# First layer's norms with operands in PSUM, and a scheduler with new durations and offsets

## The chip, the cores and the metric

The kernel runs on one core of a Trainium2 chip. A core has five engines that run their own instruction streams and meet only at semaphores: PE (TensorE, matrix products), DVE (VectorE), ACT (ScalarE), POOL (GpSimd) and SP (SyncE, which here issues nearly all DMAs). The metric is the device time of one execution in microseconds (us), as a median of several runs.

## The reference

Four images of 512 channels and 32 x 32 positions pass two layers, each added to its input:

```python
x = x + mamba(group_norm(x))      # layer 0
x = x + pab(group_norm(x))        # layer 1
```

Layer 0 takes each image as a sequence of 1024 tokens. It norms over the channels of a token, projects 512 channels to 2 x 1024, runs a causal convolution with four taps and a SiLU on one half, and from it makes `dt` (softplus), `B` and `C` (16 states each). The scan is, for each of 1024 channels and 16 states,

```python
h = exp(dt * A) * h + (dt * x) * B
y = sum over the states of h * C
```

and `(y + x * D) * silu(z)` is projected back to 512 channels. Layer 1 makes two 1x1 convolutions to 64 channels, a softmax over the whole 1024 x 1024 map, a 3x3 convolution that the map is applied to, and a last 3x3 convolution. All is float32. Both group norms have 32 groups of 16 channels.

## The kernel before, in words

Layer 0 works on tiles of 128 channels by 1024 tokens. A unit is one batch, one of eight channel tiles `d`, one of 16 states `s`: 512 units in all (function `unit`). In a unit with an even state, ACT scales the transposed `dtx` (= `dt * x`) by `B` and PE turns it into `u` in PSUM; with an odd state, SP loads the row of `B` to all partitions (`bbc`, L755) and POOL multiplies (L760). ACT makes `da = exp(dt * A)` (L739, L766), DVE scans (L774), POOL multiplies by the row of `C` (`cbc`, L786; for four states DVE does, L781), and PE adds the product into `y` (L794). So POOL has 640 products of 128x1024, and `dtx` (L689). It also transforms the weights of layer 1 in 32 filling pieces (`transform`, L1054 to L1074; ACT scales, L1046 and L1047; SP loads and stores).

Around the units stand, per batch: `norms` (both norms in one chain), `conv1` (projection `pxm`, ACT tap L584, DVE taps L593, SiLU), `gates` (`pz`, SiLU, stored to DRAM), `params` (`B`, `C`), `delta` (`dt`, `dtx`), `gate` (`pyb`, L832, L835), and `out_proj` for the batch before (loads `gt`, `wpr`, `res`; groups `po` on PE; L874). The last batch has `last_proj` instead, and `first_image` loads, norms and pads the first image for layer 1.

The norms chain: `bn_stats` on DVE; a matmul averages the means in a group (`pm`); `mid` makes the deviation; a matmul averages it (`pv`); ACT takes Ln and Exp (L247, L248) into `rstd`; `shift` makes `nb` (L444) and the matrix `mw` (L448); a matmul makes the mean shift, which is taken from `nb` (L464). Then per half of 512 tokens: group `pmu`, its DVE step (L487), ACT's squares (`sq`, L501), the group `pvar`; at last Ln and Exp (L517, L521) into `rs`, the DVE step L528 and ACT's scale and bias (L536).

The order of all this is not written out. Each piece of work is a `step` with an engine, a duration that is written in the code, what it reads and writes, and a priority (its due unit). `Plan.issue` runs a model of the five engines over these numbers and issues on each engine the ready step of lowest priority among those that can start soonest (`SLACK`); buffers come from rings with a fixed count of slots (`mm`: two PSUM buffers for all projections, turns and norms; `h` 4, `bb` 5, `cbc` 4, `wpr` 2, `res` 2, `xs` 10). `HOP` is what passes between engines, `LOAD` an ACT table load, `AHEAD` how far a filling step may run ahead. The offsets in `PRM` are due units relative to a batch: `m0` and `n0` for the norms of batch 1 and of 2 and 3, with `nl` between their parts, `q0`/`qg` and `c0`/`cg` for the convolutions of batch 1 and of 2 and 3, `e0`/`eg` and `g0`/`gg` for the gates, `o0`/`og` for the output projection, `dl` for `delta`, `fi` for the first image. A due unit decides the order alone; on the chip each engine then runs its list strictly in order.

Layer 1 has no plan: its 3x3 convolutions are matmuls over transformed weights (`m_b`, `m_o`, L1349), with `pat` and `psc` for the map.

Of the kernel before, what the change touches and what calls it, by code (L numbers as in the profile page):

```python
# [10 lines left out]
ALU = mybir.AluOpType  # L11
# [19 lines left out]
PRM = dict(fi=-0.55, m0=45.75, n0=43.74, nl=2.01, q0=54.7, qg=6.23, c0=54.63, cg=6.71, p0=120.47, e0=6.16, eg=3.72, g0=78.98, gg=9.04, o0=4.96, og=3.78, dl=8.57, t0=10, tg=20)  # L31
# [24 lines left out]
class Plan:  # L56
# [4 lines left out]
    HOP, LOAD, SLACK, AHEAD = 0.1, 1.28, 0.08, 16.23  # L61
# [41 lines left out]
    def issue(self):  # L103
# [6 lines left out]
        while left:  # L110
# [4 lines left out]
            for e in self.ENGINES:  # L115
                urgent = min((s.prio for s in ready[e] if s.table in (None, table)), default=1e9)
                found = []
                for s in ready[e]:
# [3 lines left out]
                    if s.fill and e == "DVE":  # L122
                        t = max(t, clock["POOL"])
# [25 lines left out]
            s.done = clock[s.eng] = t + s.us  # L149
            if s.fill and s.eng == "DVE":  # L150
                clock["POOL"] = max(clock["POOL"], s.done)
# [10 lines left out]
            for u in s.users:  # L162
                u.unmet -= 1
                hop = self.HOP if u.eng != s.eng or s.kb else 0.0
                u.ready = max(u.ready, s.done + hop)
                if not u.unmet:
                    ready[u.eng].append(u)
# [4 lines left out]
def mamba_then_pab_kernel(  # L172
# [76 lines left out]

    image = {}  # L250
# [5 lines left out]
    with ExitStack() as l0:  # L256
# [72 lines left out]
        MM, TR = 0.93, 0.145  # L329
# [46 lines left out]
        def norms(b, prio, lag=0.0):  # L376
# [14 lines left out]
            for c in range(NCC):  # L391

                def stats(c=c):
                    if c == 0:
                        spl["mv"] = tiny("mv", [P, NCC, 2])
                    bs = spool.tile([P, NH, 6], F32, tag="bs", name=f"bs_l0_{b}_{c}")
                    for h, hs in enumerate(halves):
                        nc.vector.bn_stats(bs[:, h, :], t()[:, c, hs])
                    nc.vector.bn_aggr(spl["mv"][:, c, :], bs)

                step("DVE", 1.6, stats, [t], [stat], prio)
# [10 lines left out]
            def mid():  # L412
                mv = spl["mv"]
                spl["mean"], spl["dev"] = tiny("gmean", [P, NCC]), tiny("gdev", [P, NCC])
                mean, dev = spl["mean"], spl["dev"]
                nc.vector.tensor_copy(mean, pm()[:, :NCC])
                nc.vector.tensor_sub(dev, mv[:, :, 0], mean)
                nc.vector.tensor_mul(dev, dev, dev)
                nc.vector.tensor_add(dev, dev, mv[:, :, 1])

            step("DVE", 0.8, mid, [pm], [stat], prio)
# [10 lines left out]
            def root():  # L432
                spl["rstd"] = tiny("grstd", [P, NCC])
                rsqrt(spl["rstd"], pv()[:, :NCC])

            step("ACT", 0.6, root, [pv], [stat], prio, "ln")

            mw = buf("res", [P, T], f"mw_{b}")  # L440

            def shift():
                spl["nb"] = tiny("gnb", [P, NCC])
                nc.vector.scalar_tensor_tensor(  # L444
                    spl["nb"], spl["mean"], -1.0, spl["rstd"], ALU.mult, ALU.mult
                )
                for c in range(NCC):
                    nc.vector.tensor_scalar_mul(  # L448
                        mw()[:, c * P : (c + 1) * P], mean_w, spl["rstd"][:, c : c + 1]
                    )  # L450

            step("DVE", 1.1, shift, [], [stat, mw], prio)

            def shift_mean():
                for c in range(NCC):
                    nc.tensor.matmul(
                        pv()[:, NCC : NCC + 1], mean_w, spl["nb"][:, c : c + 1],
# [3 lines left out]
            step("PE", 1.2, shift_mean, [stat], [pv], prio)  # L461
            step(
                "DVE", 0.3,
                lambda: nc.vector.tensor_sub(  # L464
                    spl["nb"], spl["nb"], pv()[:, NCC : NCC + 1].to_broadcast([P, NCC])
# [3 lines left out]
            rs = buf("xs", [P, L], f"rs_{b}")  # L469
            by_half = [buf(None, None, "") for h in range(NH)]  # L470
            by_chunk = [buf(None, None, "") for c in range(NCC)]
            for h, hs in enumerate(halves):
# [4 lines left out]
                            lambda c=c: mw()[:, c * P : (c + 1) * P],  # L477
# [6 lines left out]
                for c in range(NCC):  # L484
                    step(
                        "DVE", 0.7,
# [7 lines left out]
            for h, hs in enumerate(halves):  # L494
                prio += lag
                pvar = buf("mm", [P, T], f"pvar_{b}_{h}")
                for c in range(NCC):
                    sq = buf("res", [P, T], f"sq_{b}_{h}_{c}")
                    step(
                        "ACT", 0.63,  # L500
# [14 lines left out]
            def logs():  # L515
                for hs, pvar in zip(halves, pvars):
                    nc.scalar.activation(rs()[:, hs], pvar(), AF.Ln, bias=eps)  # L517

            step("ACT", 1.35, logs, pvars, [rs], prio, "ln")
            step(  # L520
                "ACT", 1.15, lambda: nc.scalar.activation(rs(), rs(), AF.Exp, scale=-0.5),  # L521
                [], [rs], prio, "exp",
            )
            prio += lag
            for c in range(NCC):
                step(
                    "DVE", 1.22,
                    lambda c=c: nc.vector.scalar_tensor_tensor(  # L528
                        t()[:, c, :], t()[:, c, :], spl["nb"][:, c : c + 1], rs(),
                        ALU.add, ALU.mult,  # L530
                    ),
                    [rs, *by_half], [by_chunk[c]], prio, holds=[t],
                )
                step(
                    "ACT", 1.15,
# [30 lines left out]
        def conv1(b, d, prio):  # L566
# [5 lines left out]
            for at, end in ((0, 341), (341, 682), (682, L)) if b else ((0, L),):  # L572
# [15 lines left out]
                step("ACT", 0.18 + n / 1000, tap, [p], [u], prio)  # L588
# [10 lines left out]
                step("DVE", 0.3 + n / 250, taps, [p], [u], prio)  # L599
            step(  # L600
                "ACT", 1.15,
# [4 lines left out]
        def gates(b, d, prio):  # L606
# [3 lines left out]
            for h, hs in enumerate(halves):  # L610
                p = project(b, NDC + d, w, f"pz_{b}_{d}_{h}", hs, prio)
                step(
                    "ACT", 0.62,
# [4 lines left out]
                "ACT", 1.15, lambda: nc.scalar.activation(sz(), sz(), AF.Silu),  # L618
# [7 lines left out]
        def params(b, prio):  # L626
# [3 lines left out]
            for h, hs in enumerate(halves):  # L630
                pp = buf("mm" if b else f"y{h}", [P, T], f"pp_{b}_{h}")
                for d in range(NDC):
# [10 lines left out]
                    "ACT", 0.58,  # L643
# [9 lines left out]
            def turn():  # L653
# [9 lines left out]
                "DVE", 0.3, lambda: nc.vector.tensor_copy(bt(), pt()[:, :, RK : RK + NS]),  # L663
# [3 lines left out]
        def delta(b, d, prio):  # L667
# [4 lines left out]
            for h, hs in enumerate(halves):  # L672
# [4 lines left out]
                    "ACT", 0.62,  # L677
# [6 lines left out]
                "ACT", 1.15, lambda: nc.scalar.activation(dt(), dt(), AF.Softplus),  # L684
# [4 lines left out]
            step("POOL", 2.38, lambda: nc.gpsimd.tensor_mul(dtx(), dt(), u()), [dt, u], [dtx], prio)  # L689
            dtxt = buf("dtxt", [P, NT, P], f"dtxt_{b}_{d}")  # L690
            for h in range(NH):
                pt = buf("mm", [P, NK, P], f"pdt_{b}_{d}_{h}")

                def turn(h=h, pt=pt):
# [8 lines left out]
                    "ACT", 0.59,  # L703
# [5 lines left out]
        def unit(b, d, s, y):  # L709
# [13 lines left out]
            if s in B_ON_ACT:  # L723
# [3 lines left out]
                for j in range(2):  # L727
# [8 lines left out]
                    step("ACT", 1.24, rows, [dtxt, bt], [sc], prio)  # L736
                step(
                    "ACT", 1.14,
# [12 lines left out]
            else:  # L751
# [8 lines left out]
                    "POOL", 2.38, lambda: nc.gpsimd.tensor_mul(dbx(), dtx(), b_bc()),  # L760
# [4 lines left out]
                    "ACT", 1.12,  # L765
# [7 lines left out]
                "DVE", 2.28,  # L773
# [5 lines left out]
            if on_dve:  # L779
                step(  # L780
                    "DVE", 1.22, lambda: nc.vector.tensor_mul(hc(), ht(), c_bc()),  # L781
                    [ht, c_bc], [hc], prio,
                )
            else:
                step(
                    "POOL", 2.38, lambda: nc.gpsimd.tensor_mul(hc(), ht(), c_bc()),  # L786
# [15 lines left out]
        def gate(b, d, y):  # L802
# [11 lines left out]
            for h, hs in enumerate(halves):  # L814
                step(
                    "ACT", 0.59,
# [3 lines left out]
            for h, hs in enumerate(halves):  # L820
# [16 lines left out]
                step("DVE", 1.45, mul, [u, sz], [p, g], prio + 2)  # L837
# [8 lines left out]
        def out_proj(b, h, prio, gap):  # L846
# [9 lines left out]
            for c in range(NCC):  # L856
# [16 lines left out]
                    "DVE", 0.68,  # L873
# [29 lines left out]
        def last_proj(ds, prio, gap):  # L903
# [9 lines left out]
            for c in range(NCC):  # L913
# [3 lines left out]
                for h, hs in enumerate(halves):  # L917
# [14 lines left out]
                        "DVE", 0.68,  # L932
# [14 lines left out]
        def first_image(prio):  # L947
# [12 lines left out]
            for c in range(NCC):  # L960
# [20 lines left out]
                step("DVE", 1.7, stats, [chunks[c]], [stat], prio + 4)  # L981
# [10 lines left out]
            def mid():  # L992
                mv = spl["mv"]
                mean, dev = (
                    spool.tile([P, NCC], F32, tag=n, name=f"{n}_image") for n in ("gmean", "gdev")
                )
                nc.vector.tensor_copy(mean, pm()[:, :NCC])
                nc.vector.tensor_sub(dev, mv[:, :, 0], mean)
                nc.vector.tensor_mul(dev, dev, dev)
                nc.vector.tensor_add(dev, dev, mv[:, :, 1])  # L1000
                spl["mean"], spl["dev"] = mean, dev

            step("DVE", 0.8, mid, [pm], [stat], prio)
# [13 lines left out]
            step("ACT", 0.6, root, [pv], [stat], prio, "ln")  # L1017
            for c in range(NCC):
                step(
                    "DVE", 0.82,  # L1020
# [491 lines left out]
```

## Time and profile before

| | |
|---|---|
| time before, median of 3 runs | 3212.28 us (3209.63 to 3219.53) |
| profiled execution, its time | 3218.39 us |
| its span | 3216.6 us, 34591 instructions |
| mean granted TensorE clock | 0.953 |
| first layer's POOL work ends | 2167.9 us |
| second layer's first `psc` matmul | 2191.3 us |
| HBM | 718.18 MB read, 96.99 MB written, 253 GB/s |

The profile gives the busy time of each engine over the span, in slices or in stretches that one asks for; lists of waits (who waited, for whom, the sum, how often, the longest); and instructions in order of time with the idle time before them and what ended it. A group's row has a count, the busy time and the mean of one. An engine's busy time does not tell what bounds the kernel: for that one needs the engine's waits in each stretch.

### The profile page before, as it was taken

Reading aid. Unit: us, or ns where it says so; the run is one execution under the profiler, and the core shown is the slowest. Engines: PE = TensorE matmul, PEld = TensorE weight load, DVE = VectorE, ACT = ScalarE, POOL = GpSimd, SP = SyncE. Lnnn points to the kernel's source line nnn. Section 1 sums busy time; section 2 is a strip of 40 time slices with the busy share of each in tenths; the row PEclk is TensorE's granted clock in tenths of the full one; section 3 lists DMA queues with packets and bytes.
Section 4 is the critical chain, followed back from the end, with each engine's and each line's share of the span. In section 5 each row is a group of like instructions: output and inputs, shape, how many; then the busy total and the mean of one; then the engine's idle time right before and its main releaser. Section 6 shows DMA issues by size and latency. Waiting matters only on the chain. (4 is left out here: it accounts for less than half of the span.)

```text
span 3216.6 us, 34591 instructions
## 1 busy us (share of the span) xinstructions
PE 2776.3 (86%) x11256; PEld 1633.3 (51%) x11256; DVE 2210.4 (69%) x1802; ACT 1897.9 (59%) x3567; POOL 2259.9 (70%) x1207
## 2 busy tenths in 40 slices
PE   5888678889788888877888877879999999999998
PEld 2355555555555555556555555554444444444443
DVE  3367898875898866789887588987365446447444
ACT  3399889986789987778998679853030030021000
POOL 8799889998979898988989899983142133224222
PEclk9999899999889999989999989989999999999999
DMA  6698778899868788977889988886448628818917
GB/s 185 190 304 307 232 228 268 296 317 310 295 205 258 263 302 309 343 242 230 266 281 310 319 272 304 280 229 227 184 157 314 235 100 310 295 50 304 327 66 253
DMA packets 404379, 817.49 MB, mean 254 GB/s; under 512 B 48232, under 2 KB 244584, under 8 KB 379624
## 3 DMA queue, kind: packets, MB, share of 16 engines
q1 hardware_dynamic: 395104, 799.72, 73.6%
q10 hardware_dynamic: 8936, 15.31, 1.3%
q8 instruction: 90, 1.47, 0.2%
q14 instruction: 89, 0.73, 0.1%
q0 software_dynamic: 160, 0.26, 0.0%
HBM read 718.18 MB, written 96.99 MB: 253 GB/s over the span
## 5 line engine op out<-in xcount | busy, mean ns | idle before, releaser
L774 DVE TENSOR_TENSOR_SCAN da<-da,u 128x1024 f32<-128x1024 f32 x256 | 581.7, 2274 | 121.2 <-PE u L745 120.7
L731 ACT ACTIVATE sc<-dtxt,bt_sb 128x128 f32<-128x128 f32 x2048 | 632.8, 390 | 44.3 <-PE u L745 44.2
L760 POOL TENSOR_TENSOR bbc<-dtx,bbc 128x1024 f32<-128x1024 f32 x256 | 605.2, 2377 | 67.3 <-DMA bbc<-bcd 42.5
L786 POOL TENSOR_TENSOR da<-da,cbc 128x1024 f32<-128x1024 f32 x256 | 608.4, 2378 | 51.1 <-DVE da L774 37.4
L794 PE MATMUL y<-ident,da 128*128 128x128 f32 x2048 | 306.3, 297 | 180.8 <-POOL da L786 178.5
L794 PEld LDWEIGHTS y<-ident,da 128*128 128x128 f32 x2048 | 250.1, 152 | 285.5 <-POOL da L786 267.1
L794 PE MATMUL y<-ident,bbc 128*128 128x128 f32 x2048 | 299.1, 293 | 72.3 <-POOL bbc L786 48.7
L739 ACT ACTIVATE da<-dt,a_sb 128x1024 f32<-128x1024 f32 x256 | 290.8, 1142 | 99.8 <-PE y L794 96.8
L774 DVE TENSOR_TENSOR_SCAN bbc<-u,bbc 128x1024 f32<-128x1024 f32 x128 | 291.9, 2280 | 79.7 <-ACT u L766 62.5
L1349 PE MATMUL m_b<-uw_b,v_b 128*128 128x512 f32 x768 | 337.2, 596 | 8.5 <-DMA uw_b<-u_b 7.5
L1349 PE MATMUL m_o<-uw_o,v_o 128*128 128x512 f32 x768 | 334.6, 596 | 4.4 <-DVE v_o L1271 4.1
L786 POOL TENSOR_TENSOR bbc<-bbc,cbc 128x1024 f32<-128x1024 f32 x128 | 302.8, 2365 | 43.4 <-DVE bbc L774 36.7
L774 DVE TENSOR_TENSOR_SCAN u<-u,bbc 128x1024 f32<-128x1024 f32 x128 | 292.1, 2282 | 59.0 <-ACT u L766 26.5
L794 PEld LDWEIGHTS y<-ident,bbc 128*128 128x128 f32 x2048 | 253.5, 152 | 139.1 <-POOL bbc L786 87.3
L745 PE MATMUL u<-ident,sc 128*128 128x128 f32 x2048 | 289.3, 287 | 36.5 <-DVE da L774 21.8
L766 ACT ACTIVATE u<-dt,a_sb 128x1024 f32<-128x1024 f32 x256 | 284.8, 1112 | 60.3 <-DVE bbc L781 30.3
L745 PEld LDWEIGHTS u<-ident,sc 128*128 128x128 f32 x2048 | 249.4, 149 | 87.5 <-issue 30.4
L369 PE MATMUL pxm<-xt,winc 128*128 128x341 f32 (+3 forms) x704 | 246.5, 494 | 18.9 <-ACT xt L536 9.9
L369 PE MATMUL pz<-xt,winc 128*128 128x512 f32 x512 | 241.0, 599 | 3.5 <-ACT dt L678 1.8
L1349 PEld LDWEIGHTS m_o<-uw_o,v_o 128*128 128x128 f32 x768 | 146.1, 191 | 191.2 <-issue 182.3
L1349 PEld LDWEIGHTS m_b<-uw_b,v_b 128*128 128x128 f32 x768 | 144.2, 191 | 194.5 <-issue 178.6
L1397 PE MATMUL pat<-y_b,st 128*128 128x512 f32 x512 | 221.7, 593 | 0.1
(220 smaller groups left out, 3925.0 us busy)
## 6 DMA issues: line engine op xcount, KB each, us to landing
cbc<-bcd SPq DMA_DIRECT2D x512, 512.0 KB, 5.5
bbc<-bcd SPq DMA_DIRECT2D x256, 512.0 KB, 6.3
uw_b<-u_b SPq DMA_DIRECT2D x96, 1024.0 KB, 4.9
uw_o<-u_o SPq DMA_DIRECT2D x96, 1024.0 KB, 4.8
u_b<-work SPq DMA_DIRECT2D x192, 128.0 KB, 2.8
u_o<-work SPq DMA_DIRECT2D x192, 128.0 KB, 4.8
winc<-in_w_in_dram SPq DMA_DIRECT2D x64, 256.0 KB, 5.2
szd<-sz SPq DMA_DIRECT2D x32, 512.0 KB, 6.4
```

The lines of the kernel that those rows point to most:

```text
L369: lambda k=k, lhs=lhs, rhs=rhs: nc.tensor.matmul(p()[:, at : at + cols], lhs(), rhs(), start=(k == 0), stop=(k == n - 1)),
L731: nc.scalar.activation(sc()[:, k, :], dtxt()[:, k, :], AF.Copy, scale=bt()[:, k, s : s + 1],)
L739: lambda: nc.scalar.activation(da(), dt(), AF.Exp, scale=scale),
L745: nc.tensor.transpose(u()[:, k * P : (k + 1) * P], sc()[:, k, :], ident)
L760: "POOL", 2.38, lambda: nc.gpsimd.tensor_mul(dbx(), dtx(), b_bc()),
L766: lambda: nc.scalar.activation(da(), dt(), AF.Exp, scale=scale),
L774: lambda: nc.vector.tensor_tensor_scan(ht(), da(), dbx(), 0.0, ALU.mult, ALU.add),
L786: "POOL", 2.38, lambda: nc.gpsimd.tensor_mul(hc(), ht(), c_bc()),
L794: nc.tensor.matmul(y[h]()[:, k, :], hc()[:, at * P : (at + 1) * P], ident, start=(s == 0 and k == 0), stop=(s == NS - 1 and k == NK - 1), ...
L1349: nc.tensor.matmul(m[q], v[:, q, k, c, :], w[:, c, :], start=(c == 0), stop=(c == NCC - 1 and not extra),)
L1397: nc.tensor.matmul(pt, st[m][:, 2 * P * j + h : 2 * P * (j + 1) : 2], xb[m // 2][:, m % 2, :], start=(m == 0), stop=(m == NMC - 1),)
```

## The change

In the norms of layer 0, DVE's small steps are rewritten so that each has one operand or its result in PSUM. A new function `deviation` is used by the norms of layer 0, by the first image and by layer 1; it does the subtraction twice, once into SBUF and once into PSUM, and multiplies the two. `rstd` is made in PSUM by ACT, `mw` by one 128x512 product with `rstd` spread over the columns instead of four 128x128 ones, and a copy of `rstd` goes to SBUF. The last Ln goes to two halves in the ring `res`, where one tile in `xs` stood, and Exp writes back into `pvar`; the last DVE step becomes two halves of 512 tokens, which read `pvar`, so that the two `pvar` buffers stay taken until these steps are done.

In the plan, the end of a step for others is now its occupancy plus a lag by engine (`LAG`), `HOP` is halved, nearly all written durations are changed, a rule that held DVE's filling steps behind POOL is dropped, and the offsets are new. Nearly every engine's list comes out in another order.

```diff
-PRM = dict(fi=-0.55, m0=45.75, n0=43.74, nl=2.01, q0=54.7, qg=6.23, c0=54.63, cg=6.71, p0=120.47, e0=6.16, eg=3.72, g0=78.98, gg=9.04, o0=4.96, og=3.78, dl=8.57, t0=10, tg=20)
+PRM = dict(fi=1.82, m0=38.64, n0=42.12, nl=2.68, q0=54.7, qg=6.23, c0=61.05, cg=6.69, p0=120.47, e0=0.92, eg=3.72, g0=78.98, gg=9.02, o0=9.88, og=3.78, dl=8.21, t0=10, tg=20)
...
-    HOP, LOAD, SLACK, AHEAD = 0.1, 1.28, 0.08, 16.23
+    LAG = {"PE": 0.2, "DVE": 0.08, "ACT": 0.1, "POOL": 0.06, "SP": 0.0}
+    HOP, LOAD, SLACK, AHEAD = 0.05, 1.3, 0.08, 15.34
...
-            s.done = clock[s.eng] = t + s.us
+            clock[s.eng] = t + s.us
+            s.done = clock[s.eng] + self.LAG[s.eng]
...
-                hop = self.HOP if u.eng != s.eng or s.kb else 0.0
-                u.ready = max(u.ready, s.done + hop)
+                other = u.eng != s.eng or s.kb
+                u.ready = max(u.ready, s.done + self.HOP if other else clock[s.eng])
...
+    def deviation(p, mv, mean, dev):
+        nc.vector.tensor_copy(mean, p[:, :NCC])
+        nc.vector.tensor_sub(dev, mv[:, :, 0], p[:, :NCC])
+        nc.vector.tensor_sub(p[:, NCC : 2 * NCC], mv[:, :, 0], p[:, :NCC])
+        nc.vector.tensor_mul(p[:, 2 * NCC : 3 * NCC], dev, p[:, NCC : 2 * NCC])
+        nc.vector.tensor_add(dev, p[:, 2 * NCC : 3 * NCC], mv[:, :, 1])
...
-        MM, TR = 0.93, 0.145
+        MM, TR = 0.88, 0.114
...
-                for c in range(NCC):
-                    nc.vector.tensor_scalar_mul(
-                        mw()[:, c * P : (c + 1) * P], mean_w, spl["rstd"][:, c : c + 1]
-                    )
-
-            step("DVE", 1.1, shift, [], [stat, mw], prio)
+                r = pv()[:, NCC : 2 * NCC]
+                nc.vector.scalar_tensor_tensor(spl["nb"], spl["mean"], -1.0, r, ALU.mult, ALU.mult)
+                nc.vector.tensor_mul(
+                    mw(), mean_w.rearrange("p (o n) -> p o n", o=1).to_broadcast([P, NCC, P]),
+                    r.rearrange("p (c o) -> p c o", o=1).to_broadcast([P, NCC, P]),
+                )
+                nc.vector.tensor_copy(spl["rstd"], r)
+
+            step("DVE", 0.9, shift, [pv], [stat, mw], prio)
...
-            step(
-                "ACT", 1.15, lambda: nc.scalar.activation(rs(), rs(), AF.Exp, scale=-0.5),
-                [], [rs], prio, "exp",
-            )
...
+            rs = [buf("res", [P, T], f"rs_{b}_{h}") for h in range(NH)]
...
+                    lambda r=r, pvar=pvar: nc.scalar.activation(pvar(), r(), AF.Exp, scale=-0.5),
+                    [r], [pvar], prio, "exp",
...
-                    "DVE", 1.22,
-                    lambda c=c: nc.vector.scalar_tensor_tensor(
-                        t()[:, c, :], t()[:, c, :], spl["nb"][:, c : c + 1], rs(),
-                        ALU.add, ALU.mult,
-                    ),
-                    [rs, *by_half], [by_chunk[c]], prio, holds=[t],
+                for h, hs in enumerate(halves):
+                    step(
+                        "DVE", 0.61,
+                        lambda c=c, hs=hs, p=pvars[h]: nc.vector.scalar_tensor_tensor(
+                            t()[:, c, hs], t()[:, c, hs], spl["nb"][:, c : c + 1], p(),
+                            ALU.add, ALU.mult,
+                        ),
+                        [pvars[h], by_half[h]], [by_chunk[c]], prio, holds=[t],
+                    )
...
-                "POOL", 2.38,
+                "POOL", 2.31,
...
-                "DVE", 2.28,
+                "DVE", 2.2,
```

## The prediction

> **What bounds the kernel now.** I read the page's engine rows first, then the busy time by stretch, then POOL's list of waits, then POOL and DVE in order of time around the longest ones.
>
> ```profile
> PE 2776.3 (86%) x11256; PEld 1633.3 (51%) x11256; DVE 2210.4 (69%) x1802; ACT 1897.9 (59%) x3567; POOL 2259.9 (70%) x1207
> ...
> 150.00:600.00 450.00, 362.15 (x1850) 249.54 (x1849) 357.30 (x265) 405.85 (x752) 408.72 (x216) 0.93 0.81 269
> 600.00:1100.00 500.00, 416.86 (x2104) 284.56 (x2102) 393.81 (x288) 414.30 (x783) 443.98 (x232) 0.93 0.83 278
> 1100.00:1600.00 500.00, 414.16 (x2125) 279.31 (x2123) 398.53 (x290) 418.16 (x796) 450.97 (x238) 0.95 0.85 282
> 1600.00:2168.00 568.00, 467.05 (x2525) 324.51 (x2523) 461.20 (x293) 459.45 (x919) 528.81 (x257) 0.94 0.86 286
> ...
> 2191.00:3216.00 1025.00, 992.78 (x2388) 443.38 (x2388) 532.44 (x582) 139.36 (x242) 293.64 (x131) 0.99 0.61 218
> ```
>
> After the mark, a row's columns are PE, weight loads, DVE, ACT, POOL, granted clock, DMA. From 2191 us on the second layer runs with PE busy 992.8 of 1025 us; little of the change touches it. Between 150 and 2168 us, the first layer's scans, POOL leads: 1832.5 of 2018 us, 91%, always the busiest. Its work there is the same in both programs, so the layer shortens by POOL waits that disappear (2018 - 1832.5 = 185.5 us) and POOL operations that are no longer stretched.
>
> ```profile
> POOL bbc L760 <- DMA bbc<-bcd: 42.5, 21, 9.9
> POOL da L786 <- DVE da L774: 37.4, 24, 3.4
> POOL bbc L786 <- DVE bbc L774: 36.7, 16, 4.9
> ...
> POOL bbc L760 <- PE po L369: 9.4, 1, 9.4
> ...
> POOL bbc L786 <- DVE gnb_l L444: 5.8, 1, 5.8
> POOL da L786 <- DVE gnb_l L464: 4.8, 2, 3.9
> ```
>
> Two kinds matter: late B rows from SP's queue (9.9, 9.4 and, at 1266 us, 7.4), and scans that come late because DVE is inside the norms.
>
> ```profile
> 338.65 2.12 DVE L417 TENSOR_TENSOR gdev_l<-mv_l,gmean_l 128x4 f32<-128x4 f32 x1
> 340.80 2.27 DVE L418 TENSOR_TENSOR gdev_l<-gdev_l 128x4 f32<-128x4 f32 x1
> 343.10 2.27 DVE L419 TENSOR_TENSOR gdev_l<-gdev_l,mv_l 128x4 f32<-128x4 f32 x1
> ...
> 351.01 5.09 DVE L448 TENSOR_SCALAR mw<-mean_w,grstd_l 128x128 f32<-128x128 f32 x4
> ...
> 371.04 2.71 DVE L487 SCALAR_TENSOR_TENSOR xt<-xt,grstd_l,pmu 128x512 f32<-128x512 f32 x4
> ...
> 1444.58 10.09 DVE L528 SCALAR_TENSOR_TENSOR xt<-xt,gnb_l,rs 128x1024 f32<-128x1024 f32 x4 [0.46 <-ACT rs L521]
> ...
> 1444.71 3.37 POOL L786 TENSOR_TENSOR da<-da,cbc 128x1024 f32<-128x1024 f32 x1
> ...
> 1453.55 1.71 POOL L1072 TENSOR_TENSOR work<-work 128x256 f32<-128x256 f32 x1
> 1455.34 0.72 POOL L1073 TENSOR_TENSOR work<-work 128x256 f32<-128x256 f32 x1
> ```
>
> A 128x4 step with both operands in SBUF takes up to 2.3 us, a whole POOL operation, while L487, with an operand in PSUM, takes 0.68 us a piece under the same busy POOL. L528 holds POOL up as well: its 0.72 us steps take 1.6 to 1.7, its 2.36 us product 3.37.
>
> **Part 1: norms of batches 1 to 3.** Per batch, three deviation steps (6.7, 5.7 and 2.6 us), L444 and L448 (5.2, 3.3, 5.6) and four L528 (7.2, 11.2, 10.1) come to 19.1, 20.2 and 18.3 us of DVE. The new form is four small steps for three, one 128x512 product for four 128x128, one more small copy, and eight 128x512 steps for four 128x1024. At 0.14 us for a small step from PSUM (L464: 126 to 158 ns) and 0.68 us for a 128x512 one (L487), that is 6 x 0.14 + 9 x 0.68 = 7.0 us. DVE gains 11 to 13 us a batch. DVE is not the bound (79 to 81% busy), so the worth is what POOL lost: waits right behind these steps of 5.8, 2.6 (near 345), 2.6, 3.2, 3.4 (877 to 935), 2.5 and 3.9 us (1396 to 1412), together 24.0; and stretching of 3.7, 3.0 and 3.8 us, together 10.5. That is 34.5. Eight steps in a row still hold DVE 5.4 us, and the L487 groups remain, so some lateness stays: 3 us a batch. Worth: 34.5 - 9 = 25 us.
>
> The Trainium skill speaks against this: Perfetto Trace Analysis, section Optimizing Scalar/DVE Operations, gives a DVE instruction about 60 ns of access overhead on SBUF and about 125 ns on PSUM. In this trace the small copy from PSUM (L416) reads 135 to 163 ns and the SBUF step L418 161 ns where POOL leaves it alone. By the rule, 15 DVE steps a batch cost 15 x 65 ns = 1 us more, 3 us over three batches, making 22 for 25. I take the rows, and keep the 3 us for the upper end.
>
> **Part 2: SP's order around the output projection.** The offsets move the projection of the batch before about 5 units later (o0 4.96 to 9.88), its `gt`, `wpr` and `res` loads and stores with it, past other B and C row loads. A `wpr` load waits for the PE group before last (two buffers); every load behind it on SP waits too, and POOL's product L760 waits for that load. I counted, in both programs' order of instructions, how many units lie between the PE step that SP must have passed before a B row is issued and that row's use on POOL. In before the smallest leads are 3.9, 4.7 and 5.0 units, and these rows are exactly the stalls of 9.4, 7.4 and 9.9 us, 26.7 together. Rows with 6.2 to 8.6 show no such stall. In the changed program the smallest lead is 6.9. I credit 22 of 26.7. The projection also changes on PE: before has runs of 24, 16 and 16 uninterrupted matmuls (the 24 take 20.8 us), after has six of 16 (13.8 us each). Two runs of 16 before cost POOL 2.4 and 1.5 us beyond SP's lateness; six at 2 us are 12, against 2.4 + 1.5 + 3.1 (behind the 24) = 7: minus 5. Net worth: 17 us.
>
> **Part 3: the end of the layer.** Before, the last two C rows stand between the first image's slow loads on SP (four take 7.83 us, the C rows issue at 2151.7 and 2154.0), and POOL waits 4.6 and 4.5 us. After, all C rows stand ahead of the eight image loads. POOL ends 9 us earlier, but loads, statistics and image norm follow later: about 15 us for the loads, then 1.4 for the last statistics and 4 us to the root, against the 9 us from POOL's end to the root now. The scans in front of the two waits are late too (DVE had waited 1.9 us for `po` and then did statistics), so the rows explain only part. I take 4 of 9 us.
>
> **Part 4: costed at nothing.** *First norm of batch 0*: the deviation ends about 1 us sooner, but ACT is on filling steps until 25.94 and only then loads its table. The wide product is hidden by the four matmuls of L456 (1.9 us). The halved last step gives chunk 0 about 0.5 us later and chunk 3 about 1 us earlier. Together between +1 and -1.5. *ACT tables*: 186 loads become 178, 8 x 1.28 = 10 us of ACT, beside POOL; at most 2 us where ACT feeds a scan. *Exp into PSUM*: no row shows a 128x512 one; half of L521's 1060 ns is the nearest, against 684 for L517, so 0 to +0.3 us a batch. *Two PSUM buffers held longer*: `pvar` now lasts until DVE's eight steps, some 8 us more a batch; what waits is the next `pd`, `pdt` and `pyb`. `dt` is planned 8 units (some 30 us) ahead, which covers it; without cover it costs 8 us, 24 in all. *Second layer*: small steps of 0.16 us beside `pat`; nothing. *Gates of batch 0* 5 units earlier, *norm of batch 1* 7 earlier, *projections of batches 2 and 3* 6.4 later with their weight loads: their price is in the discount below.
>
> **Sum.** 25 + 17 + 4 = 46 us of POOL. Not all arrives: an earlier POOL meets the next late row, scan or `h` tile, and the fresh order deals the remaining 130 us of waits anew. From nothing I can count is that fraction exact; I take three quarters, 35 us. The profiled execution took 3218.4 us (span 3216.6 and 1.8 around it): 3218.4 - 35 = 3183. The median, 3212.3, is 6.1 lower: 3177.
>
> **Rivals.** *The new bookings do more (0.21).* The plan books a scan at 2.2 and a POOL product at 2.31 us, which is the spacing in the trace (2.20 and 2.31) where it had 2.28 and 2.38; copies go from 0.6 to 0.48. If the order fits the chip everywhere, half of the remaining 130 us goes too: 3177 - 60 = 3117. For: 24 and 16 small waits for scans in the list above. Against: a uniform 3% error leaves an order unchanged.
>
> *All given back (0.07).* The waits reappear elsewhere: 3209, within 10 us of now.
>
> *Slower: the projection's runs on PE (0.11).* Six runs of 13.8 us keep `y` adds back, so `h` tiles stay taken and ACT cannot start `da` (it sat 8 to 11 us behind such runs). If each run of 16 costs POOL what the 24 did with its SP lateness, 7.4 + 3.1 = 10.5 us, six cost 63 rather than 12: 51 more, against 35 gained: 3228. It decides from about 35 / 6 + 2 = 8 us a run. Against it: two such runs cost 2.4 and 1.5.
>
> **How the numbers follow.** Main case 0.61, 3157 to 3196, time 3177. About 0.3% (10 us) is what a measurement can tell from no change. Faster by more: 0.61 + 0.21 + 0.02 of the given-back case = 0.84; the same 0.05; slower 0.11. The range 3125 to 3211 leaves out the lowest part of the first rival and the slower one; the 3 us of the rule and the 24 us of held buffers lie inside it.
>
> **What would show it.** Right: deviation steps of 0.1 to 0.2 us, the wide product near 0.65, the last norm step near 0.7 under any POOL load; no POOL step over 2.5 us in the first layer; no POOL wait for a B row over 6 us; POOL's end near 2130 us, the second layer again about 1025 us. Wrong: POOL waiting 8 us or more at several projection runs, long waits of `dtx` for `dt` after a norm, or a second layer that changed by over 10 us.

## The result, and the profile after

| | before | after |
|---|---|---|
| time, us (median of 4 runs each) | 3210.95 (3208.60 to 3219.53) | 3175.05 (3173.59 to 3183.09) |
| ratio | | 0.9889, 95% interval 0.9864 to 0.9913 |
| span of the profiled execution, us | 3216.6 | 3171.8 |
| POOL's last product of the first layer ends, us | 2167.9 | 2118.6 |
| first scores of the second layer on PE, us | 2191.3 | 2148.5 |
| from there to the end, us | 1025.3 | 1023.3 |

The kernel became 36 us faster by the medians, 45 us by the two profiled executions. All of it comes from the first layer; the second is as long as it was. The forecast time, 3177 us, is 2 us off. The next sections show that its parts were less good than its sum.

The engine row of the page, and the rows of busy time by stretch (columns as before: PE, weight loads, DVE, ACT, POOL, granted clock, DMA share, GB/s):

```profile
PE 2761.5 (87%) x11256; PEld 1645.2 (52%) x11256; DVE 2160.3 (68%) x1818; ACT 1882.7 (59%) x3563; POOL 2247.5 (71%) x1207
...
150.00:600.00 450.00, 376.26 (x1960) 265.95 (x1959) 362.23 (x277) 422.13 (x786) 423.68 (x224) 0.94 0.84 279
600.00:1100.00 500.00, 423.61 (x2142) 293.10 (x2141) 390.59 (x298) 420.70 (x809) 455.51 (x242) 0.92 0.86 287
1100.00:1600.00 500.00, 421.00 (x2157) 289.54 (x2156) 397.35 (x305) 415.74 (x800) 453.60 (x241) 0.94 0.85 287
1600.00:2120.00 520.00, 428.21 (x2343) 303.11 (x2343) 422.62 (x261) 419.66 (x847) 489.38 (x236) 0.93 0.86 287
```

POOL is still the busiest engine in every stretch. It works 1822.2 of 1970 us, 92.5%, and is idle for 147.8 us where it was idle for 185.5. DVE is 50 us lighter, with 16 instructions more. POOL's list of waits up to 2190 us:

```profile
POOL da L802 <- DVE da L790: 45.3, 33, 4.9
POOL bbc L802 <- DVE bbc L790: 23.7, 17, 4.7
...
POOL bbc L776 <- DMA bbc<-bcd: 19.9, 9, 5.5
POOL dtx L705 <- ACT dt L700: 17.8, 8, 9.3
POOL work L1065 <- ACT work L1057: 17.8, 4, 6.4
```

The late B rows went from 21 waits with 42.5 us to 9 with 19.9, the longest from 9.9 to 5.5. No wait put down to one of DVE's norm steps is left anywhere in this list. The waits for scans hardly shrank (45.3 + 23.7 = 69.0 us, before 37.4 + 36.7 = 74.1), and those for `dtx` and for the filters' input grew (17.8 each, before 13.5 and 11.5).

DVE in order of time at the norm of batch 1, where before had 2.12, 2.27, 2.27 and 5.09 us:

```profile
320.06 0.15 DVE L252 TENSOR_TENSOR gdev_l<-mv_l,pm_l 128x4 f32<-128x4 f32 x1
320.12 0.16 DVE L253 TENSOR_TENSOR pm_l<-mv_l,pm_l 128x4 f32<-128x4 f32 x1
320.32 0.17 DVE L254 TENSOR_TENSOR pm_l<-gdev_l,pm_l 128x4 f32<-128x4 f32 x1
320.52 0.16 DVE L255 TENSOR_TENSOR gdev_l<-pm_l,mv_l 128x4 f32<-128x4 f32 x1
...
328.32 0.68 DVE L457 TENSOR_TENSOR mw<-mean_w,pv_l 128x512 f32<-128x512 f32 x1
```

Each small step has one operand in PSUM, and it takes the same time under a busy POOL as alone: over its seven calls in both layers L252 takes 148 to 149 ns, L254 166 to 167.

At the end of the layer some of the gain is given back. POOL ends 49.3 us earlier, the first scores come 42.9 us earlier. SP's queue and ACT in order of time:

```profile
2105.66 14.01 SPq L981 DMA_DIRECT2D xg<-x  x8
...
2131.50 0.63 ACT L1166 ACTIVATE brow_b<-brow_b 1x512 f32<-1x512 f32 x1 [8.52 <-DMA brow_b<-in_b_bottom_dram]
2132.27 0.63 ACT L1166 ACTIVATE brow_o<-brow_o 1x512 f32<-1x512 f32 x1
2132.92 1.28 ACT L245 ACT_TABLE_LOAD   x1
2134.21 0.26 ACT L245 ACTIVATE grstd_image<-pv_image,eps 128x4 f32<-128x4 f32 x1
```

The eight image loads now stand together behind the last C row (14.01 us), and in ACT's order the bias rows of the second layer stand ahead of the image's root, with 8.52 us of waiting for their DMA. Before, they stood behind the root.

### The profile page after: what moved, and what is told of

Its sections match the earlier page's. It is cut to its first block, busy times and chain, and to the rows that moved or that the text cites. A ratio compares the mean times of both kernels' runs of the same rounds, so it can differ in the third digit from the quotient of the medians.

```text
span 3171.8 us, 34608 instructions
## 1 busy us (share of the span) xinstructions
PE 2761.5 (87%) x11256; PEld 1645.2 (52%) x11256; DVE 2160.3 (68%) x1818; ACT 1882.7 (59%) x3563; POOL 2247.5 (71%) x1207
## 5 line engine op out<-in xcount | busy, mean ns | idle before, releaser
L802 POOL TENSOR_TENSOR da<-da,cbc 128x1024 f32<-128x1024 f32 x256 | 606.0, 2368 | 57.7 <-DVE da L790 45.3
L776 POOL TENSOR_TENSOR bbc<-dtx,bbc 128x1024 f32<-128x1024 f32 x256 | 603.7, 2371 | 28.3 <-DMA bbc<-bcd 19.9
L810 PE MATMUL y<-ident,da 128*128 128x128 f32 x2048 | 299.3, 293 | 88.4 <-POOL da L802 81.3
L810 PEld LDWEIGHTS y<-ident,bbc 128*128 128x128 f32 x2048 | 261.4, 154 | 134.5 <-POOL bbc L802 55.3
L802 POOL TENSOR_TENSOR bbc<-bbc,cbc 128x1024 f32<-128x1024 f32 x128 | 302.9, 2367 | 26.5 <-DVE bbc L790 23.7
L376 PE MATMUL pxm<-xt,winc 128*128 128x345 f32 (+3 forms) x704 | 251.1, 503 | 23.5 <-DVE xs L609 9.4
```

The source lines that it names most:

```text
L376: lambda k=k, lhs=lhs, rhs=rhs: nc.tensor.matmul(p()[:, at : at + cols], lhs(), rhs(), start=(k == 0), stop=(k == n - 1)),
L776: "POOL", 2.31, lambda: nc.gpsimd.tensor_mul(dbx(), dtx(), b_bc()),
L802: "POOL", 2.31, lambda: nc.gpsimd.tensor_mul(hc(), ht(), c_bc()),
L810: nc.tensor.matmul(y[h]()[:, k, :], hc()[:, at * P : (at + 1) * P], ident, start=(s == 0 and k == 0), stop=(s == NS - 1 and k == NK - 1), ...
```

## The experiments

All runs were made beside the kernel before on the same chip. Ratios are to it. The medians of before differ by up to 6.5 us between the sittings (the one of the result had 3210.95), so runs of different sittings are compared by their ratios; 0.001 is 3.2 us.

| run | time, us (range) | ratio, 95% interval |
|---|---|---|
| small steps from PSUM, order of before | 3197.23 (3196.34 to 3198.87) | 0.9944, 0.9926 to 0.9963 |
| all norm steps in SBUF, new order | 3208.34 (3203.29 to 3219.38) | 0.9976, 0.9968 to 0.9984 |
| last step in SBUF, new order | 3200.03 (3196.16 to 3205.62) | 0.9955, 0.9937 to 0.9972 |
| five B rows earlier, in before | 3216.60 (3208.89 to 3225.63) | 1.0002, 0.9994 to 1.0010 |
| projection spread | 3174.89 (3170.68 to 3182.46) | 0.9870, 0.9854 to 0.9885 |
| bias rows later | 3177.28 (3173.52 to 3181.44) | 0.9879, 0.9862 to 0.9895 |
| image loads earlier | 3182.51 (3178.03 to 3185.81) | 0.9890, 0.9875 to 0.9905 |
| offsets of before | 3205.59 (3201.92 to 3209.52) | 0.9963, 0.9950 to 0.9976 |
| small steps in SBUF, new order | 3186.48 (3183.88 to 3189.84) | 0.9912, 0.9895 to 0.9929 |
| bookings of before | 3246.21 (3242.37 to 3252.49) | 1.0100, 1.0080 to 1.0119 |
| spread and bias rows together | 3182.21 (3171.66 to 3183.78) | 0.9892, 0.9870 to 0.9913 |
| changed kernel again | 3179.65 (3177.19 to 3180.39) | 0.9888, 0.9870 to 0.9906 |

The first four stood beside a median of 3216.5 us for before, the next four beside 3217.5, the last four beside 3215.2.

### Small steps alone, in the order of before

```diff
-                nc.vector.tensor_sub(dev, mv[:, :, 0], mean)
-                nc.vector.tensor_mul(dev, dev, dev)
-                nc.vector.tensor_add(dev, dev, mv[:, :, 1])
+                nc.vector.tensor_sub(dev, mv[:, :, 0], p[:, :NCC])
+                nc.vector.tensor_sub(p[:, NCC : 2 * NCC], mv[:, :, 0], p[:, :NCC])
+                nc.vector.tensor_mul(p[:, 2 * NCC : 3 * NCC], dev, p[:, NCC : 2 * NCC])
+                nc.vector.tensor_add(dev, p[:, 2 * NCC : 3 * NCC], mv[:, :, 1])
...
-                for c in range(NCC):
-                    nc.vector.tensor_scalar_mul(
-                        mw()[:, c * P : (c + 1) * P], mean_w, spl["rstd"][:, c : c + 1]
-                    )
+                nc.vector.tensor_mul(
+                    mw().rearrange("p (c n) -> p c n", n=P),
+                    mean_w.rearrange("p (o n) -> p o n", o=1).to_broadcast([P, NCC, P]),
+                    r.rearrange("p (c o) -> p c o", o=1).to_broadcast([P, NCC, P]),
+                )
```

> The kernel before, its order and offsets untouched; only the small norm steps (deviation, nb, mw) take an operand in PSUM, the last step L528 stays in SBUF. Theory A (half from the forms, half from SP's order): the waits of 5.8, 2.6, 2.5 and 3.9 us behind these steps go, some 14 us of POOL, of which three quarters arrive: 10 us less, 3201. Theory B (the forms do it all): 25 to 36 less, 3175 to 3186. Theory C (the new order does it all, the forms are hidden): within 5 us of 3211.

Measured: 3197.23 us, 19 below the median of before beside it. POOL and SP have the same order as before, so the start of each POOL instruction can be compared one by one: it comes earlier by 8.5 us more at 315 to 366 us, 5.5 at 828 to 930 and 5.6 at 1339 to 1446, at the three norms. These make 19.6 us; between the norms the lead drifts by some 2 us, and at the layer's end it is 21.7 (22 us of span). What POOL saved at a norm arrived. The last step was left in SBUF, and its row in the groups of DVE shows why there was more to get:

```profile
L530 DVE SCALAR_TENSOR_TENSOR xt<-xt,gnb_l,rs 128x1024 f32<-128x1024 f32 x16 | 39.1, 2502 | 13.1 <-ACT rs L523 13.1
...
L447 DVE TENSOR_TENSOR mw<-mean_w,pv_l 128x512 f32<-128x512 f32 x4 | 2.7, 679 | 0.0
```

### All norm steps back in SBUF, in the new order

The forms of the small steps as in before; the last step keeps its halves and its place, and reads a tile in SBUF:

```diff
-                    lambda r=r, pvar=pvar: nc.scalar.activation(pvar(), r(), AF.Exp, scale=-0.5),
+                    lambda hs=hs, r=r: nc.scalar.activation(rsx()[:, hs], r(), AF.Exp, scale=-0.5),
...
-                            t()[:, c, hs], t()[:, c, hs], spl["nb"][:, c : c + 1], p(),
+                            t()[:, c, hs], t()[:, c, hs], spl["nb"][:, c : c + 1], rsx()[:, hs],
```

> The changed kernel with the same order on POOL and SP, but every norm step back to operands in SBUF (deviation, nb, four mw products, last step from SBUF). Theory A: 15 to 20 us above the changed kernel, 3190 to 3195. B: 3211, all is lost. C: 3175, as the changed kernel.

Measured: 3208.34 us, 8 below before. With the norms in SBUF the new order is worth only that. Against the changed kernel (0.9976 for 0.9889) the forms of all norm steps are worth 28 us in this order. POOL and SP have the changed kernel's order; on the other engines four single steps changed places.

### Only the last step in SBUF, in the new order

The two edits shown above, nothing else.

> The changed kernel with only the last norm step (eight of 128x512) reading its rs from SBUF; the small steps stay in PSUM. Theory A: POOL is stretched again by 3 to 4 us per batch and the next scan comes 3 us later: 6 to 10 us above the changed kernel, 3183. B: 3187 or more. C: 3175.

Measured: 3200.03 us, by the ratios (0.9955 for 0.9889) 21 above the changed kernel. DVE's groups in this run and in the changed kernel (busy us, mean ns):

```profile
L545 DVE SCALAR_TENSOR_TENSOR xt<-xt,gnb_l,rsx 128x512 f32<-128x512 f32 x32 | 44.8, 1464 | 13.0 <-ACT rsx L537 13.0
```

```profile
L544 DVE SCALAR_TENSOR_TENSOR xt<-xt,gnb_l,pvar 128x512 f32<-128x512 f32 x32 | 21.5, 741 | 11.8 <-ACT pvar L536 11.8
```

One operand moved from PSUM to SBUF doubles the mean of an otherwise equal instruction beside a busy POOL. By POOL's starts the loss is 5.0 us in batch 0, 6.0 near 383 us, 6.9 near 900, 4.0 near 1400, and it stays (25.1 at the layer's end). Batch 0 is the surprise. POOL in order of time there, first in the kernel before, then in the changed one:

```profile
60.07 1.71 POOL L1072 TENSOR_TENSOR work<-work 128x256 f32<-128x256 f32 x1
61.86 1.59 POOL L1073 TENSOR_TENSOR work<-work 128x256 f32<-128x256 f32 x1
63.52 1.59 POOL L1074 TENSOR_TENSOR work<-work 128x256 f32<-128x256 f32 x1
65.07 1.71 POOL L1072 TENSOR_TENSOR work<-work 128x256 f32<-128x256 f32 x1
```

```profile
58.90 0.73 POOL L1083 TENSOR_TENSOR work<-work 128x256 f32<-128x256 f32 x1
59.71 0.73 POOL L1084 TENSOR_TENSOR work<-work 128x256 f32<-128x256 f32 x1
```

Four steps of 0.73 us took 1.59 to 1.71 in before, 3.7 us over. No scan runs yet, but POOL's filters do, and they are part of the same total.

This run is not quite the form of before: eight halves in SBUF took 9.96 us of DVE in batch 0, before's four whole rows 7.34. Over four batches it is 44.8 us here against 7.34 + 7.2 + 11.2 + 10.1 = 35.8 in before and 21.5 after. If POOL's loss goes with DVE's time, the last step against its own form of before is worth (35.8 - 21.5) / (44.8 - 21.5) = 0.61 of 21 us, an estimate of 13.

### Only the small steps in SBUF, in the new order

The deviation, the root and the four products of `mw` as in before, the last step from PSUM.

> The changed kernel with the order of POOL and SP unchanged and the small steps of the first layer's norms (deviation, L456, the wide product as four, the root into SBUF) in the forms of before; the last step keeps its operand in PSUM. If the two groups of steps cost POOL independently, the time is the changed kernel's plus what lies between the two runs that had only the last step (3200) and all of them (3208) in SBUF: 8 us, about 3183. If the small steps are worth here what they were worth in the order of before, it is 18 us more: about 3193. If the group that comes first uses up the slack and the other one then costs little, 3178.

Measured: 3186.48 us, 7 above the changed kernel run beside it (3179.65); the intervals of the two ratios overlap, but the profiles say the same: POOL ends the layer 5.2 us later (2126.9 for 2121.7). DVE's groups:

```profile
L466 DVE TENSOR_SCALAR mw<-mean_w,grstd_l 128x128 f32<-128x128 f32 x16 | 13.0, 872 | 0.0
L425 DVE TENSOR_TENSOR gdev_l<-gdev_l 128x4 f32<-128x4 f32 x4 | 4.2, 1052 | 0.1
L424 DVE TENSOR_TENSOR gdev_l<-mv_l,gmean_l 128x4 f32<-128x4 f32 x4 | 4.1, 1033 | 0.1
```

The steps are stretched here too, but less: the three of the deviation take 9.0 us over the four batches, in before 16.4. And what POOL loses does not all stay. Against the changed kernel beside it, POOL falls behind by 6.0 us at 331 to 380, by 2.9 near 884 and by 4.8 near 1385; 4.2 come back by 1400, and of the 13.7 only 5.2 are left at the layer's end. So the same edit is worth 19 us in the old order and about 7 in the new one: its worth depends on the order around it. 7 and 21 make the 28 of the run with both groups in SBUF.

### Five B rows earlier, in the kernel before

```diff
+EARLY = [((3, 1, 9), (3, 1, 4)), ((2, 1, 7), (2, 1, 4)), ((0, 6, 13), (0, 6, 7)), ((1, 1, 9), (1, 1, 4)), ((1, 4, 7), (1, 4, 2))]
...
+        for row, ahead in EARLY:
+            a = next(i for i, (s, _) in enumerate(order) if s and s.name == ("B", *row))
+            z = next(i for i, (s, _) in enumerate(order) if s and s.name == ("C", *ahead))
+            order.insert(z, order.pop(a))
```

> The kernel before, with five of SP's 1700 rows moved: the loads of the B rows (3,1,9), (2,1,7), (0,6,13), (1,1,9) and (1,4,7), each taken ahead of the two C row loads that hold it (a C row waits for a slot that POOL itself frees, so the B row behind it was issued 2.3 us or less of POOL work before its use). Theory A: POOL's waits of 9.9, 9.4 and 7.4 us shrink by 5 us each or more and two smaller ones go: 12 to 20 us less, 3191 to 3199. Theory B: no change, 3211. Theory C: 12 to 20 less as well, but then e1 gains nothing. A buffer of the bb ring that isn't free earlier would leave it at 3211.

Measured: 3216.60 against 3216.51 us, nothing. The three stalls shrank (9.86 to 4.50, 7.42 to 2.88, 9.39 to 5.85). POOL in order of time at the first, in before and in this run:

```profile
759.42 2.36 POOL L760 TENSOR_TENSOR bbc<-dtx,bbc 128x1024 f32<-128x1024 f32 x1 [9.86 <-DMA bbc<-bcd]
...
769.57 2.35 POOL L760 TENSOR_TENSOR bbc<-dtx,bbc 128x1024 f32<-128x1024 f32 x1 [0.86 <-DMA bbc<-bcd]
```

```profile
752.75 2.35 POOL L773 TENSOR_TENSOR bbc<-dtx,bbc 128x1024 f32<-128x1024 f32 x1 [4.50 <-DMA bbc<-bcd]
755.05 2.37 POOL L799 TENSOR_TENSOR bbc<-bbc,cbc 128x1024 f32<-128x1024 f32 x1
760.31 2.36 POOL L799 TENSOR_TENSOR da<-da,cbc 128x1024 f32<-128x1024 f32 x1 [2.90 <-DVE da L787]
765.27 2.35 POOL L799 TENSOR_TENSOR da<-da,cbc 128x1024 f32<-128x1024 f32 x1 [2.60 <-DVE da L787]
771.10 2.36 POOL L773 TENSOR_TENSOR bbc<-dtx,bbc 128x1024 f32<-128x1024 f32 x1 [3.48 <-DMA bbc<-bcd]
```

POOL goes on 6.7 us earlier and meets two scans that are not ready and the next B row. By that row, which starts at 769.57 before and 771.10 here, the lead is gone. The long stall had covered other work that was equally late.

### Projection spread over its gap

```diff
-                            out_proj(b - 1, h, at + PRM["o0"] + 4 * PRM["og"] * h, PRM["og"])
+                            out_proj(b - 1, h, at + PRM["o0"] + (4 * PRM["og"] + 6) * h, PRM["og"])
```

and in `group` each matmul is due `gap * k / n` later than the first; uninterrupted runs of ten and more matmuls fall from 96 to 11.

> The changed kernel with the output projection's eight matmuls of a group due one after the other over the group's gap (og), not all at once, and its second half six units later; runs of ten or more uninterrupted po matmuls on PE fall from 96 to 11 matmuls. e4 showed that waits for B rows in the projection come back as waits for scans when the rows are earlier. Theory D: PE's runs are behind them, since y adds stand still and the h tiles stay taken; of some 50 us of POOL's idle time around the three projections 15 to 25 go: 3150 to 3160. Rival E: these waits have other causes (the late gt load, ACT): 3175, within 5.

Measured: 3174.89 us, ratio 0.9870: no different from the changed kernel within the intervals. POOL idles less around the three projections (35.3 us for 46.9, from a projection's first matmul to 5 us after its last), but as much up to its last product of the layer (173.1 for 171.3). So the projection's runs on PE are not what holds the layer.

### The end of the layer: bias rows later, image loads earlier

```diff
         st, rp = scores(0, xg)
+        brow = []
+        for name, src in (("b", b_bottom), ("o", b_out)):
...
```

with the same lines taken from their old place; in the other kernel `fi` goes from 1.82 to -0.55.

> The changed kernel with the loads and scaling of the two bias rows of layer 1 put after the first scores. In the changed kernel ACT waits 8.5 us for such a row, then does the Ln of the first image's norm at 2134.2, 2 us after its matmul. Theory: the Ln starts at its matmul, 2 us less: 3173. Rival: PE's last projection groups set the end there: 3175.

> The changed kernel with the first image's offset of before (fi -0.55 for 1.82): its loads stand among the last C rows on SP again. By the prediction's part 3 the move was worth 4 us: 3179. Rival: nothing, since what POOL gains before its end is lost in the 6.5 us that the stretch behind it grew: 3175.

Measured: with the bias rows later the root starts at 2131.8 for 2134.2 us and the first scores at 2146.1 for 2148.5, yet the span is 3171.7 for 3171.8: the second layer takes the 2.4 us back. With the image loads earlier the time is 3182.51 us, 0.9890: no difference. Both edits at once with the spread, as a candidate to beat the changed kernel:

> Both edits at once, the projection's matmuls spread over their gap and the bias rows loaded after the first scores: a version that could beat both kernels. If the 15 us that the spread took from POOL's idle time around the projections can be kept, 3160 to 3168. If what is saved there goes into other waits and the second layer takes back the earlier start, as in the two runs with one edit each, it is the changed kernel's time, 3172 to 3178.

Measured: 3182.21 us, 0.9892, beside 3179.65 and 0.9888 for the changed kernel. None of these beats it beyond the intervals.

> The changed kernel once more, as a measure for the three others on the same chip: 3173 to 3183, 0.987 to 0.991 of the kernel before.

### Offsets of before, or bookings of before

The `PRM` line of before in the changed kernel; and in the other kernel all durations, the hop, the look-ahead and the coupling of fills of before with the new `PRM`:

```diff
-    LAG = {"PE": 0.2, "DVE": 0.08, "ACT": 0.1, "POOL": 0.06, "SP": 0.0}
-    HOP, LOAD, SLACK, AHEAD = 0.05, 1.3, 0.08, 15.34
+    LAG = {"PE": 0.0, "DVE": 0.0, "ACT": 0.0, "POOL": 0.0, "SP": 0.0}
+    HOP, LOAD, SLACK, AHEAD = 0.1, 1.28, 0.08, 16.23
...
-                "DVE", 2.2,
+                "DVE", 2.28,
```

> The changed kernel with all offsets (PRM) of before; the forms, the durations and lags are the new ones. e2 put the whole new order at 8 us with the old forms. Theory F: the offsets carry little, the durations and forms the rest: 3175 to 3182. Rival G: the offsets carry the order's part: 3185 to 3200.

> The changed kernel with its forms and its new offsets, but the planner books the durations, the hop, the table load and the look-ahead of before, no lags, and ties DVE's filling steps to POOL again. If the new bookings carry part of the gain by themselves, the time is 10 to 20 us above the changed kernel's, 3185 to 3195. If only the forms and the offsets count (a uniform error of some per cent leaves an order as it is), it is within 4 us of it, 3171 to 3180. If offsets and bookings fit only each other, it is as far above as the kernel with the old offsets was, some 25 to 30 us: 3200 to 3206.

Measured: 3205.59 us with the old offsets, 3246.21 with the old bookings, the latter 1% slower than the kernel before although all norms read PSUM. POOL's waits with the old offsets, then with the old bookings:

```profile
POOL da L802 <- DVE da L790: 70.2, 43, 8.9
POOL bbc L776 <- DMA bbc<-bcd: 45.8, 21, 10.0
```

```profile
POOL bbc L780 <- DMA bbc<-bcd: 98.1, 32, 9.6
POOL da L806 <- DVE da L794: 55.9, 32, 8.9
```

None of my three cases for the old bookings reached that far. The instruction orders suggest a reason. A B row's load stands on SP behind loads of C rows, and such a load waits until POOL or DVE has freed one of four C buffers. I added up POOL's booked work between the product that frees the buffer for the last C row ahead and the product that needs the B row (under 5 us are two products or fewer):

| order | B rows with under 5 us of POOL's work between | POOL's waits for B rows, us |
|---|---|---|
| before | 20 | 42.5 |
| changed | 7 | 19.9 |
| offsets of before | 15 | 45.8 |
| bookings of before | 26 | 98.1 |

Few rows short of lead go with little waiting. That is a correlation of four orders. It does not name a price for a row, and moving five of them by hand brought nothing.

## Why the prediction was right, and where it was not

**The sum was right, and its closeness is luck.** The forecast had 19 us from the norms (25 times three quarters), 13 from SP's order and 3 from the end of the layer. What the norms are worth depends on what is counted first. Order first: the new order alone gives 8 us, the norm forms in it 28, an upper bound, as the last step is cut finer than in before; with the estimate for before's own form it is 7 + 13 = 20, which leaves 16 for the order. Forms first: the small steps alone gave 19 in the order of before, and the stretching of POOL beside the last step in that trace, 10.5 us in batches 1 to 3 and 3.7 in batch 0, makes about 33 (an estimate), which leaves 3. So the norms are worth 20 to 33 us and the order 3 to 16; the forecast of 19 and 16 stands at one end of that. That the total hit within 2 us came from terms that were too small (the small steps, batch 0), one that came to nothing (the end of the layer) and a factor that had been assumed.

**Part 1, the right mechanism, with steps mis-sized.** Three are shown. First, "costed at nothing: first norm of batch 0" looked only at DVE's chain to the first scan. POOL's filters run beside it, and the four rows of 1.59 to 1.71 us stood in the trace of before: 3.7 us, counted for batches 1 to 3 and left out here. Secondly, the factor of three quarters. In the order of before the gains at the norms stayed to the end; in the new order the small steps keep 5.2 of 13.7 us, the last step all of it. There is no one factor. Thirdly, the small steps alone, in the order of before: 14 us of waits were expected to go and 10 to arrive, and they gave 19 even with the last step's stretching left. The durations themselves were right: 0.15 to 0.17 us for the small steps, 0.68 for the wide product, 0.74 for the last step, no 128x1024 product on POOL over 2.50 us (before 3.37).

**The rule that spoke against.** The extra time of an operand in PSUM did not show: 0.148 to 0.167 us beside the 0.161 us that a step in SBUF takes when POOL leaves it alone. Taking the rows was right. What the PSUM operand removes fits the Trainium skill, SBUF — State Buffer, section SBUF: two separate sides: a DVE instruction with two SBUF inputs and a POOL instruction take one port pair, and the one that starts first keeps it for its whole instruction. A 128x4 step of 2.27 us is then one of POOL's products, which come every 2.31 us, waited out. The runs show the waiting, not the port.

**Part 2, the right place with the wrong account.** B rows did come less late, as forecast (no wait over 6 us; 5.5). But the 22 of 26.7 us took each stall as worth its length. The run with five rows moved shows a stall standing in front of other late work: 13.4 us less waiting at three places, nothing gained. The cause that I named, `wpr` loads that wait for the projection's PE groups and hold SP, is not the main one. SP's own waits between 150 and 2200 us, in before and in the changed kernel (C rows at L718 and L734, `wpr` at L894 and L910):

```profile
SPq L718 <- POOL da L786: 500.4, 218, 8.2
SPq L718 <- POOL bbc L786: 251.3, 118, 7.6
...
SPq L894 <- PE po L369: 18.9, 15, 3.3
```

```profile
SPq L734 <- POOL da L802: 391.8, 177, 8.6
SPq L734 <- POOL bbc L802: 222.8, 105, 6.1
...
SPq L910 <- PE po L376: 40.6, 13, 6.9
```

SP waits for C buffers many times longer than for `wpr`, and its wait for `wpr` doubled while the late B rows halved. Most of SP's waiting costs nothing, as it runs ahead of POOL, which waits for B rows for 42.5 and 19.9 us in all; but what changed with the late rows over four orders is the lead behind the C buffers.

**Part 3.** POOL ended the layer 11 us earlier than the 2130 forecast, and 6.4 us of that went in the stretch up to the first scores (23.4 us before, 29.9 after). The 4 us credited for this end did not show: with the first image back at its old offset the ratio is 0.9890 for 0.9889, and the later bias rows brought nothing either. What lengthened the stretch stays open.

**Part 4.** Exp into PSUM takes 0.594 us, and into SBUF (the run with the last step there) 0.623: no cost. Table loads fell to 178 as forecast. `dtx` waited 17.8 us for `dt` instead of 13.5, far from 24; in the two runs that give the buffers back after Exp it still waited 16.1 and 15.6, so the held buffers account for some 2 us. For the second layer the prediction read small steps of 0.16 us; one of them, L1182, took 2.34 us in each of three images and takes 0.15 now. The layer still moved by only 2 us, its PE being busy nearly throughout.

**The rivals.** "Slower through the projection's runs" did not come, and the spread shows that the runs don't set the time. "The new bookings do more" reckoned with 130 us of remaining waits; 185.5 of idle time less the waits among the 46 leave about 150. It was argued down with the remark that a uniform error leaves an order unchanged. But the error was not uniform: the scan's booking fell from 2.28 to 2.2 us, ACT's copies from as much as 0.62 to 0.48. And the runs show that bookings matter: the bookings alone, with all else kept, make 67 us (3179.65 to 3246.21), the offsets alone 24 by the ratios (0.9963 for 0.9889). Neither is a gain in itself: new offsets with old bookings are slower than before, old offsets with new bookings give up most of the gain. That the pair as a whole is worth 3 to 16 us over before could not have been read from the trace of before.

**What stays open.** Between 20 and 33 us for the norms, since no run had before's whole rows in the new order, nor the last step from PSUM in the old one. Why the old bookings with the new offsets lose 67 us is shown only as a correlation with the lead of the B rows. The changed kernel's two profiled executions, 3171.8 and 3178.6 us of span, differ by 7 us, some 3 of it near 1800 us; differences below that between single profiles mean little.

## What to carry to other kernels

When one engine bounds a stage, add up how long its own instructions take beside each kind of neighbour: a small step on another engine may be off the critical path and still hold up the bound engine, from the first phase on. Changing where such a neighbour's operand lies is worth whole microseconds, all of which arrived in one order here and a good third for the small steps in the other. A long stall is worth only what is not also late behind it: look at the next two or three instructions before crediting it. Where a planner sets the order, offsets and booked durations are one setting, and neither is tried or judged without the other.

## What was not expected of the hardware

The same DVE instruction, 128x512 with its operand in SBUF instead of PSUM, went from 741 to 1464 ns on average (721 to 749 against 727 to 2849), and POOL's 128x256 steps beside it from 0.73 to 1.05 to 1.17 us, against 1.59 to 1.71 beside the 128x1024 form: both engines are slowed, not one. DVE and POOL in batch 0 of the run with the last step in SBUF, and DVE there in before:

```profile
57.96 9.96 DVE L545 SCALAR_TENSOR_TENSOR xt<-xt,gnb_l,rsx 128x512 f32<-128x512 f32 x8 [12.98 <-ACT rsx L537]
60.53 1.17 POOL L1084 TENSOR_TENSOR work<-work 128x256 f32<-128x256 f32 x1
61.78 1.05 POOL L1085 TENSOR_TENSOR work<-work 128x256 f32<-128x256 f32 x1
```

```profile
58.86 7.34 DVE L528 SCALAR_TENSOR_TENSOR xt<-xt,gnb_l,rs 128x1024 f32<-128x1024 f32 x4 [13.31 <-ACT rs L521]
```

Both engines step at one pace there: six DVE steps of 1.21 us beside six filters that start 1.16 us apart, and in before steps of 1.74 us beside filters that start 1.67 us apart, as if the two took turns. How much a 128x4 step in SBUF loses depends on where it falls: L418 took 2.27 to 2.29 us in batches 1 to 3 of before, the same step 0.64 to 2.27 us in the new order, and 0.16 us where POOL leaves it alone.
